# The opening of the x3 stage: a row broadcast moved into the stage before, a maximum given to GpSimd, the first gates ahead of a reciprocal, and k's first two pieces spread from SBUF

## The chip, the cores and the metric

The kernel runs on one core of a Trainium2 chip. The metric is the device time of one execution in microseconds (us). PE is the matrix engine, DVE the vector engine, ACT the activation engine, POOL is GpSimd, SP issues most DMAs. A core's program is one instruction stream per engine; the streams wait for each other by semaphores.

## The reference

Four residual layers follow one another on an image x of 256 x 256 positions with 128 channels: an attention along rows, two triangle multiplications, and a convolution block. Only the third layer, which makes x3 out of x2, matters here. Cut to what is computed (gn is a group norm over the image, whose statistics the kernel folds into weights):

```
z  = gn(x2)
zn = layernorm(z)                                  # over the 128 channels
a  = sigmoid(zn @ Wga + bga) * (zn @ Wla + bla)
b  = sigmoid(zn @ Wgb + bgb) * (zn @ Wlb + blb)
k  = einsum('bimc,bmjc->bijc', a, b)               # one 256x256x256 product per channel c
x3 = x2 + sigmoid(zn @ Wgo + bgo) * (layernorm(k) @ Wlo + blo)
```

## The kernel before

Data lies with the 128 channels on the partitions and the 65,536 positions along the free axis, cut into 32 pieces of 2048 positions (SC). Three stages make x3:

- **p5** (lines 1082 to 1217) makes a and b piece by piece and stores them to aD and bD. The row 1/sigma of zn goes to rs2D. Normalised pieces p5_zn live in three buffers. At its end PE multiplies pieces 30 and 31 for their output gates (line 1213), which are kept in the tiles gate_30 and gate_31.
- **p6**, "the planes" (lines 1249 to 1288), loops over the 128 channels c. Four channels of a and b are one load each (`load6`, tiles p6_A and p6_B, three buffers each). PE turns a's plane (`tri_turn`, line 1899), multiplies (`tri_multiply`, line 1910), ACT copies the product into p6_K (line 1278) and squares it into p6_sq (line 1280), DVE adds it to k1 (line 1281), POOL adds the square to k2 (line 1282). Every fourth step SP stores four channels to kD. k1 and k2 have 512 positions on each of the 128 partitions, so that piece s of 2048 positions lies on the partitions 4s to 4s+3.
- **p7** (lines 1309 to 1434) loops over the 32 pieces. For each: `gate7` multiplies x2 by a weight on PE, DVE adds a column and multiplies by the broadcast row 1/sigma (line 1347), ACT takes the sigmoid (line 1348); `spread_z` is POOL's broadcast of that row from one partition to all 128 (line 1331); `spread_k` is the broadcast of k's 1/sigma by PE (`broadcast_rows`, line 1073); `normalise_k` multiplies k by it on DVE (line 1326); `product7` multiplies by Wlo on PE; DVE combines it with the gate (line 1408), POOL adds x2 (line 1431), ACT takes sums for the next norm, SP stores x3.

Between p6 and the loop of p7 stands a prologue (lines 1375 to 1399). It turns k1 and k2 into 1/sigma of k: `k1 * k1 * (-1/D)` (line 1380), `k2 + k1` (1381), the maximum with 0 (1382), all on DVE; the square root on ACT (1383); the reciprocal on DVE into k1 (1384). k1 is stored to rkD and loaded again as rk, with piece s on the partitions s, 32+s, 64+s and 96+s, one quarter of 512 positions on each (lines 1385 to 1387). `broadcast_rows` makes four matmuls out of it: each takes the 32 partitions of its own quarter. Then the gates of pieces 0, 1 and 2 follow, and the loop runs three pieces ahead with its gates (AHEAD).

The order of the work in p5, p6 and p7 is written out by hand: each engine runs its instructions in the order of the text. All loads and stores of these stages are on SP's queue, in that order too.

The DVE instructions of the prologue stand in the text ahead of the gates, so DVE runs lines 1380 to 1384 before it takes the first gate out of the buffers p7_pm (two of them, in PSUM). `spread_z` has two buffers p7_rb in the pool p7.

Pools of SBUF tiles are laid one behind the other, a pool's tiles in the order of their first use, and a tile waits until what lay on its bytes has been read. Behind the two gate tiles (from byte 98016 of each partition) p5 has: p5_m2 2 KB, p5_var 4 KB, then p5_zn at 120544, 128736 and 136928, p5_a, p5_b. Buffers are taken in the order first, third, second: piece 29 lies on 128736, piece 30 on 120544, piece 31 on 136928. When p5 is closed, the pool rk takes its place from 114400: rk 2 KB, rs2_ 8 KB, k1 2 KB, k2 2 KB, to 128736. p6's tiles begin there, p6_A first, and later p7's: p7_junk, p7_k four times, p7_rb twice, p7_g five times, the first p7_g at 186208.

Of the kernel before, what the change touches and what calls it, by code (L numbers as in the profile page):

```python
# [9 lines left out]
F32 = mybir.dt.float32  # L10
AF = mybir.ActivationFunctionType
ALU = mybir.AluOpType
# [4 lines left out]
P = 128  # L17
N = 256
D = 128
T = N * N  # L20
SC = 2048
NSC = T // SC
CK = 512
# [9 lines left out]
def kernel(ctx: ExitStack, tc: tile.TileContext, a: dict, out: bass.AP):  # L33
    nc = tc.nc
# [116 lines left out]
    sel = const.tile([P, 32], F32, name="sel")  # L151
# [85 lines left out]
    with tc.tile_pool(name="x0", bufs=1, reuse_waits="tile") as xres, tc.tile_pool(name="p0", bufs=3, reuse_waits="tile") as sb:  # L237
# [168 lines left out]
        with tc.tile_pool(name="p1", bufs=2, reuse_waits="tile") as wk_sb, tc.tile_pool(name="p1ps", bufs=4, space=PSUM, reuse_waits="tile") as ps, tc.tile_pool(name="p1pe", bufs=1, space=PSUM, reuse_waits="tile") as psE:  # L406
# [7 lines left out]
            with tc.manual_schedule():  # L414
# [5 lines left out]
                for i, s in enumerate(order):  # L420
# [4 lines left out]
                    for c in range(4):  # L425
                        nc.tensor.matmul(
                            pr[32 * c : 32 * c + 32, :], lhsT=wt, rhs=xc[:, c * CK : (c + 1) * CK],
                            start=True, stop=True,
# [17 lines left out]
                    while len(sums) > (i < NSC - 1):  # L446
                        j, sq = sums.pop(0)
                        for c in range(4):
                            nc.tensor.matmul(
                                e2[32 * c : 32 * c + 32, :], lhsT=slide[:, 31 - j : 63 - j],  # L450
                                rhs=sq[:, c * CK : (c + 1) * CK], start=(j == order[0]), stop=(j == order[-1]),
# [24 lines left out]
    with tc.tile_pool(name="p2e", bufs=6, reuse_waits="tile") as eb, tc.tile_pool(name="p2c", bufs=1, reuse_waits="tile") as cs:  # L476
        triT = cs.tile([P, NH, 2, N], F32, name="triT")
        with tc.tile_pool(name="p2", bufs=2, reuse_waits="tile") as sb, tc.tile_pool(name="p2S", bufs=2, space=PSUM, reuse_waits="tile") as psS, tc.tile_pool(name="p2z", bufs=1, space=PSUM, reuse_waits="tile") as psZ, tc.tile_pool(name="p2M", bufs=3, space=PSUM, reuse_waits="tile") as psM, ExitStack() as by_hand:
# [182 lines left out]
            rb = psS.tile([P, 2, CK], F32, name="p2i_rb", tag="p2_S")  # L661
            for c in range(2):
                nc.tensor.matmul(
                    rb[:, c, :], lhsT=sel[32 * c : 32 * c + 32, 0:1].to_broadcast([32, P]),
                    rhs=rs0[32 * c : 32 * c + 32, :], start=True, stop=True,
# [173 lines left out]
    with x1_scope:  # L839
        with tc.tile_pool(name="p3", bufs=3, reuse_waits="tile") as sb, tc.tile_pool(name="p3ps", bufs=3, space=PSUM, reuse_waits="tile") as ps, tc.manual_schedule():  # L840
# [14 lines left out]
            for i, s in enumerate(order1):  # L855
                p1 = ps.tile([P, CK], F32, name="p3_1")
                p2 = ps.tile([P, CK], F32, name="p3_2")
                for pp, w in ((p1, v1), (p2, v2)):
                    for c in range(4):
                        nc.tensor.matmul(  # L860
                            pp[32 * c : 32 * c + 32, :], lhsT=w, rhs=xs[s][:, c * CK : (c + 1) * CK],
                            start=True, stop=True,
# [83 lines left out]
        with tc.tile_pool(name="p4", bufs=3, reuse_waits="tile") as sb, tc.tile_pool(name="p4psg", bufs=2, space=PSUM, reuse_waits="tile") as psg, tc.tile_pool(name="p4psz", bufs=2, space=PSUM, reuse_waits="tile") as psz, tc.manual_schedule():  # L946
            zs, gts, sums = {}, {}, []
# [42 lines left out]
            for i, s in enumerate(order):  # L990
# [5 lines left out]
                for c in range(4):  # L996
# [3 lines left out]
                        start=True, stop=True,  # L1000
# [67 lines left out]
    def broadcast_rows(psX, rows, s, name, tag="x"):  # L1068


        rb = [psX.tile([P, 2, CK], F32, name=name, tag=tag) for _ in range(2)]
        for c in range(4):
            nc.tensor.matmul(
                rb[c // 2][:, c % 2, :], lhsT=sel[32 * c : 32 * c + 32, s : s + 1].to_broadcast([32, P]),
                rhs=rows[32 * c : 32 * c + 32, :], start=True, stop=True,
            )
        return [t.rearrange("p c t -> p (c t)") for t in rb]
# [6 lines left out]
    gates = {s: rs2_pool.tile([P, SC], F32, name=f"gate_{s}") for s in (NSC - 2, NSC - 1)}  # L1084
# [143 lines left out]
    rk_pool = rs2_scope.enter_context(tc.tile_pool(name="rk", bufs=1, reuse_waits="tile"))  # L1228
    rk = rk_pool.tile([P, CK], F32, name="rk")
    rs2 = rk_pool.tile([P, SC], F32, name="rs2_")  # L1230

    def row7(s):
        at = 32 * (s % 4)
        return rs2[at : at + 1, :]

    def load_row7(s):
        if s < NSC - 2:
            nc.sync.dma_start(row7(s), rs2D[:, s * SC : (s + 1) * SC])

    k1 = rk_pool.tile([P, 2 * N], F32, name="k1")  # L1240
    k2 = rk_pool.tile([P, 2 * N], F32, name="k2")
    xs7 = {}

    def load7x(s):
        if s < NSC:
# [3 lines left out]
    with tc.tile_pool(name="p6", bufs=3, reuse_waits="tile") as sb, tc.tile_pool(name="p6ps", bufs=3, space=PSUM, reuse_waits="tile") as ps:  # L1249
        nc.vector.memset(k1, 0.0)  # L1250
        nc.gpsimd.memset(k2, 0.0)  # L1251
        with tc.manual_schedule():
            quads = {}

            def load6(q):
                if q < D // 4:
                    A = sb.tile([P, 4, 2 * N], F32, name="p6_A")
                    nc.sync.dma_start(A, aD[:, 4 * q : 4 * q + 4, :])
                    B = sb.tile([P, 4, 2 * N], F32, name="p6_B")
                    nc.sync.dma_start(B, bD[:, 4 * q : 4 * q + 4, :])  # L1260
                    quads[q] = A, B

            def turn6(c):
                return tri_turn(nc, ps, sb, quads[c // 4][0], c % 4, ident, nc.vector.tensor_copy)

            for q in range(3):
                load6(q)
            for s in range(4):
                load_row7(s)
            at = turn6(0)  # L1270
            for c in range(D):
                q = c // 4
                if c % 4 == 0:
                    K = sb.tile([P, 4, 2 * N], F32, name="p6_K")
                nxt = turn6(c + 1) if c + 1 < D else None
                pz = tri_multiply(nc, ps, at, quads[q][1], c % 4).rearrange("p t n -> p (t n)")
                at = nxt
                nc.scalar.copy(K[:, c % 4, :], pz)  # L1278
                sq = sb.tile([P, 2 * N], F32, name="p6_sq")
                nc.scalar.activation(sq, pz, AF.Square)  # L1280
                nc.vector.tensor_tensor(k1, pz, k1, ALU.add)  # L1281
                nc.gpsimd.tensor_tensor(k2, k2, sq, ALU.add)  # L1282
                if c % 4 == 3:
                    nc.sync.dma_start(kD[4 * q : 4 * q + 4, :].rearrange("c (p t) -> p c t", p=P), K)
                    del quads[q]
                    load6(q + 3)
                    if q >= D // 4 - 3:
                        load7x(q - (D // 4 - 3))
# [18 lines left out]
    g1 = const.tile([P, NSC + 1], F32, name="g1")  # L1307
    g2 = const.tile([P, NSC + 1], F32, name="g2")
    with tc.tile_pool(name="p7", bufs=2, reuse_waits="tile") as sb, tc.tile_pool(name="p7psX", bufs=2, space=PSUM, reuse_waits="tile") as psX, tc.tile_pool(name="p7psM", bufs=2, space=PSUM, reuse_waits="tile") as psM, tc.manual_schedule():
        ks, rks, rbs, gts = {}, {}, {}, dict(gates)  # L1310
        junk = sb.tile([P, SC], F32, name="p7_junk", bufs=1)
        AHEAD = 3

        def load7k(s):
            if s < NSC:
                ks[s] = sb.tile([P, SC], F32, name="p7_k", bufs=4)
                nc.sync.dma_start(ks[s], kD[:, s * SC : (s + 1) * SC])

        def spread_k(s):
            if s < NSC:  # L1320
                rks[s] = broadcast_rows(psX, rk, s, "p7_rk")

        def normalise_k(s, h):
            if s < NSC:
                hs = slice(h * H2, (h + 1) * H2)
                nc.vector.tensor_tensor(ks[s][:, hs], rks[s][h], ks[s][:, hs], ALU.mult)

        def spread_z(s):
            if s < NSC and s not in gates:
                rbs[s] = sb.tile([P, SC], F32, name="p7_rb")  # L1330
                nc.gpsimd.partition_broadcast(rbs[s], row7(s))

        def product7(src, w, h):
            pm = psM.tile([P, 2, CK], F32, name="p7_pm")
# [5 lines left out]
        def gate7(s, h):  # L1340
            if s < NSC and s not in gates:
                hs = slice(h * H2, (h + 1) * H2)
                if h == 0:
                    gts[s] = sb.tile([P, SC], F32, name="p7_g", bufs=5)
                pg = product7(xs7[s], wf2[:, 4, :], h)
                zg = gts[s][:, hs]
                nc.vector.scalar_tensor_tensor(zg, pg, gcol, rbs[s][:, hs], ALU.add, ALU.mult)
                nc.scalar.activation(zg, zg, AF.Sigmoid, bias=b2w[:, 4:5])
# [25 lines left out]

        load7k(0)
        load7x(3)
        spread_z(0)
        spread_z(1)

        nc.vector.scalar_tensor_tensor(k1, k1, -1.0 / D, k1, ALU.mult, ALU.mult)  # L1380
        nc.vector.tensor_tensor(k2, k2, k1, ALU.add)
        nc.vector.tensor_scalar(k2, k2, 0.0, None, ALU.max)
        nc.scalar.activation(k2, k2, AF.Sqrt, bias=epst, scale=1.0 / D)
        nc.vector.reciprocal(k1, k2)
        nc.sync.dma_start(rkD.rearrange("o (p t) -> p (o t)", p=P), k1)
        for c in range(4):
# [2 lines left out]
            load7k(s)  # L1389
        load7x(4)  # L1390
        for s in range(3):
            gate7(s, 0)
            gate7(s, 1)
            if s < 2:
                spread_z(s + 2)
                load_row7(s + 4)
        spread_k(0)
        normalise_k(0, 0)
# [1 line left out]
        for s in range(NSC):  # L1400
            load_row7(s + 6)
            load7k(s + 3)
            last = s == NSC - 1
            for h in range(2):
                hs = slice(h * H2, (h + 1) * H2)
                gate7(s + AHEAD, h)
                pl = product7(ks[s], w2[:, 5, :], h)
                nc.vector.scalar_tensor_tensor(
                    pl if last else gts[s][:, hs], pl, b2w[:, 5:6], gts[s][:, hs], ALU.add, ALU.mult
                )  # L1410
                if h == 0:
                    spread_k(s + 1)
                    spread_z(s + AHEAD + 1)
                normalise_k(s + 1, h)
                if last:
                    nc.vector.tensor_tensor(xs7[s][:, hs], pl, xs7[s][:, hs], ALU.add)
                    if h == 0:
                        finish7(s - 1)
                    for c in range(2):
                        k = 2 * h + c  # L1420
                        nc.vector.bn_stats(st7[:, k, :], xs7[s][:, k * CK : (k + 1) * CK])
                    nc.sync.dma_start(x3T[:, s * SC + h * H2 : s * SC + (h + 1) * H2], xs7[s][:, hs])
            del ks[s]
            if last:
                stats7()
            elif s == NSC - 2:
                for h in range(2):
                    hs = slice(h * H2, (h + 1) * H2)
                    nc.gpsimd.tensor_tensor(xs7[s][:, hs], xs7[s][:, hs], gts[s][:, hs], ALU.add)
            else:  # L1430
                nc.gpsimd.tensor_tensor(xs7[s], xs7[s], gts[s], ALU.add)
            if s and not last:
                finish7(s - 1)
            load7x(s + 5) if s + 5 < NSC else load9(s + 5 - NSC)
# [517 lines left out]
```

## Time and profile before

| what | us |
|---|---|
| median of three runs | 3272.09 |
| lowest and highest | 3267.91, 3276.04 |
| profiled execution: its own time | 3273.64 |
| profiled execution: span, first to last instruction | 3271.7 |
| last gate matmuls of p5 end, ACT takes them | 2333.36 |
| first turn of p6, first product of p6 on PE | 2335.88, 2338.47 |
| a step of p6 (line 1281, 128 of them) | 2.2465 |
| last step of p6 on DVE | 2628.75 |
| reciprocal, start and length | 2636.47, 3.35 |
| first matmul of gate 3, of gate 4 | 2651.66, 2659.90 |
| a step of p7, pieces 1 to 26 | 8.13 |
| first matmul after the x3 stage | 2906.44 |

Times within an execution are counted from its first instruction. A line of the timeline gives start, length, engine, source line, operation, out<-in, shape, how many were merged, and in brackets how long the engine had been idle and who ended that. A line of the table of stages gives for each engine its busy time and number of instructions, then the clock granted to PE (1.00 is full), the share of the DMA engines' time and GB/s.

### The profile page before, as it was taken

The numbers are of one execution on the slowest core, as the hardware profiler recorded it, in microseconds if no ns is written. First come the engines' busy times: TensorE is split into PE (matmuls) and PEld (weight loads), VectorE is DVE, ScalarE is ACT, GpSimd is POOL, SyncE is SP. The second block draws the span as 40 slices with busy tenths as digits, with TensorE's granted clock in tenths as the row PEclk, the third lists the DMA queues.
The fourth block names the chain that finished last, engine by engine and source line by source line (L and its number), as shares of the span: only waits on it lengthen the run. The fifth ranks groups of instructions, "written<-read, shape, count | busy, mean of one in ns | idle before, by whom it ended". The sixth has DMA issues, their size and how long they took to land. (4 is left out here: it accounts for less than half of the span.)

```text
span 3271.7 us, 51718 instructions
## 1 busy us (share of the span) xinstructions
PE 3040.7 (93%) x19792; PEld 1629.4 (50%) x19792; DVE 2248.5 (69%) x2540; ACT 2033.8 (62%) x2270; POOL 1773.4 (54%) x1019
## 2 busy tenths in 40 slices
PE   5678999999999999997799799999999989979998
PEld 4524555555555555552433244444699933324444
DVE  5626888888888888883456454454455588858887
ACT  3576777777777777763467545444344457757776
POOL 4055777777777777770268000000255568848887
PEclk8899999999999999998999899999999999989999
DMA  9982333333333333329679678666699989976775
GB/s 362 363 326 94 120 113 111 118 111 111 118 111 112 120 109 116 119 100 394 227 308 410 255 255 307 256 249 262 260 351 352 351 313 388 390 286 194 233 231 154
DMA packets 294802, 749.18 MB, mean 229 GB/s; under 512 B 71127, under 2 KB 142185, under 8 KB 245369
## 3 DMA queue, kind: packets, MB, share of 16 engines
q1 hardware_dynamic: 282671, 731.12, 61.9%
q0 software_dynamic: 9040, 13.17, 1.1%
q8 instruction: 158, 2.59, 0.3%
q10 hardware_dynamic: 2840, 1.54, 0.2%
q14 instruction: 93, 0.76, 0.1%
HBM read 458.07 MB, written 287.64 MB: 228 GB/s over the span
## 5 line engine op out<-in xcount | busy, mean ns | idle before, releaser
L555 DVE TENSOR_TENSOR p_e<-p_S,triT 128x1024 f32<-128x1024 f32 x512 | 609.4, 1212 | 144.8 <-PE p_S L545 144.8
L565 POOL TENSOR_TENSOR p_es<-p_e 128x1024 f32<-128x1024 f32 x256 | 602.8, 2367 | 126.2 <-issue 66.7
L563 ACT ACTIVATE p_e<-p_e,mbT 128x1024 f32<-128x1024 f32 x512 | 552.1, 1138 | 61.6 <-DVE p_e L555 61.6
L1154 PE MATMUL p_pm<-p_zn,wf 128*128 128x512 f32 x1040 | 448.7, 593 | 1.9 <-ACT p_a L1189 1.9
L530 PE MATMUL p_mm<-p_xn,w 128*128 128x512 f32 x768 | 405.1, 611 | 0.3 <-DVE p_v L525 0.3
L1154 PEld LDWEIGHTS p_pm<-p_zn,wf 128*128 128x128 f32 x1040 | 196.8, 190 | 253.9 <-issue 247.0
L545 PE MATMUL p_S<-p_q,p_k 32*128 32x256 f32 x4096 | 295.3, 401 | 3.5 <-DVE p_e L555 3.3
L1251 POOL MEMSET k<- 128x512 f32 x1 | 0.5, 525 | 522.4 <-PE p_pm L1154 522.4
L545 PEld LDWEIGHTS p_S<-p_q,p_k 32*128 32x128 f32 x4096 | 185.8, 184 | 159.5 <-PE p_mm L521 91.7
L504 POOL TENSOR_TENSOR p_xn<-p_xn,p_rs 128x1024 f32<-128x1024 f32 x63 | 151.3, 2401 | 205.1 <-ACT p_xn L499 108.4
L1910 PE MATMUL tp_z<-p_B,tp_at 128*128 128x256 f32 x1024 | 250.8, 388 | 0.9 <-DMA p_B<-bD 0.6
L578 PE MATMUL p_o<-p_e,p_v 128*32 128x256 f32 x4096 | 248.6, 383 | 0.0
L1282 POOL TENSOR_TENSOR k<-k,p_sq 128x512 f32<-128x512 f32 x128 | 163.1, 1274 | 136.5 <-ACT p_sq L1280 136.5
L1910 PEld LDWEIGHTS tp_z<-p_B,tp_at 128*128 128x128 f32 x1024 | 185.1, 191 | 21.9 <-DVE tp_at L1901 1.6
L530 PEld LDWEIGHTS p_mm<-p_xn,w 128*128 128x128 f32 x768 | 125.9, 190 | 104.4 <-issue 88.6
L1281 DVE TENSOR_TENSOR k<-tp_z,k 128x512 f32<-128x512 f32 x128 | 88.5, 692 | 127.0 <-ACT p_sq L1280 127.0
L578 PEld LDWEIGHTS p_o<-p_e,p_v 128*32 128x32 f32 x4096 | 120.3, 110 | 110.3 <-ACT p_g L536 41.5
L1278 ACT COPY p_K<-tp_z 128x512 f32<-128x512 f32 x128 | 74.9, 585 | 155.4 <-PE tp_z L1910 155.4
L536 ACT ACTIVATE p_g<-p_mm,bgh 128x512 f32<-128x512 f32 x128 | 87.9, 687 | 131.4 <-PE p_mm L530 131.4
L1193 DVE SCALAR_TENSOR_TENSOR p_b<-p_pm,b2w,p_b 128x1024 f32<-128x1024 f32 x64 | 82.2, 1284 | 121.7 <-PE p_pm L1154 107.3
L534 ACT ACTIVATE p_k<-p_mm,cqkg 128x512 f32<-128x512 f32 x128 | 87.9, 687 | 125.1 <-PE p_mm L530 124.9
L521 PEld LDWEIGHTS p_mm<-w,p_xn 128*128 128x128 f32 x1024 | 134.4, 191 | 61.1 <-issue 60.4
(386 smaller groups left out, 6101.2 us busy)
## 6 DMA issues: line engine op xcount, KB each, us to landing
p_x<-x2T SPq DMA_DIRECT2D x60, 1024.0 KB
x<-x1T SPq DMA_DIRECT2D x51, 1024.0 KB
p_x<-in_x_dram SPq DMA_DIRECT2D x32, 1024.0 KB
p_x<-xT SPq DMA_DIRECT2D x64, 512.0 KB
x2T<-x SPq DMA_DIRECT2D x32, 1024.0 KB
aD<-p_a SPq DMA_DIRECT2D x32, 1024.0 KB
bD<-p_b SPq DMA_DIRECT2D x32, 1024.0 KB
p_A<-aD SPq DMA_DIRECT2D x32, 1024.0 KB
```

The source lines that it names most:

```text
L504: nc.gpsimd.tensor_tensor(xn, xn, groups[g]["rs"], ALU.mult)
L521: nc.tensor.matmul(pm[:, k * D : (k + 1) * D], lhsT=t["xn"][:, b * P : (b + 1) * P], rhs=wf[:, 2 * D : 3 * D], start=True, stop=True,)
L530: nc.tensor.matmul(pm, lhsT=w, rhs=t["xn"][:, cs_], start=True, stop=True)
L545: nc.tensor.matmul(Ss[h // 2][:, h % 2, u, :], lhsT=t["k"][hp, r * N + u * P : r * N + (u + 1) * P], rhs=t["q"][hp, r * N : (r + 1) * N], ...
L555: nc.vector.tensor_tensor(e[:, :, 2 * p : 2 * p + 2, :].rearrange("p u h n -> p h u n"), Ss[p], triT[:, 2 * p : 2 * p + 2, :, :], ALU.add,)
L563: nc.scalar.activation(e[:, u, :, :], e[:, u, :, :], AF.Exp, bias=mbT[:, u, i : i + 1])
L565: nc.gpsimd.tensor_tensor(es, e[:, 0, :, :], e[:, 1, :, :], ALU.add)
L578: nc.tensor.matmul(t["o"][hp, r % 2, :], lhsT=t["v"][:, r * 2 + u, hp], rhs=e[:, u, h, :], start=(u == 0), stop=(u == 1),)
L1154: nc.tensor.matmul(pm[:, c, :], lhsT=wf2[:, i, :], rhs=zns[s][:, k * CK : (k + 1) * CK], start=True, stop=True)
L1281: nc.vector.tensor_tensor(k1, pz, k1, ALU.add)
L1282: nc.gpsimd.tensor_tensor(k2, k2, sq, ALU.add)
L1910: nc.tensor.matmul(pz[:, t, :], lhsT=at[:, u, t * P : (t + 1) * P], rhs=Bc[:, u, :], start=(u == 0), stop=(u == 1))
```

## The change

- The broadcast of row 0 is issued on POOL within p6, in step c = 112 of 128 (D - 16). Its buffer lies in the pool rk.
- `spread_z` takes the pool as an argument. Even pieces use one buffer p7_rb in the pool rk, odd ones one buffer in p7, in place of two in p7.
- In the prologue the broadcasts of rows 0 and 1 ahead of DVE's chain are gone; row 1's comes on POOL behind the maximum.
- The maximum with 0 goes from DVE to POOL.
- The gates of piece 0 (matmuls, line 1347 on DVE, sigmoid on ACT) stand ahead of the reciprocal in the text.
- k's 1/sigma for the pieces 0 and 1 is broadcast from k1 itself (`broadcast_k1`): four matmuls, all with the partitions 0 to 31 as their input, each selecting row 4s+c. Pieces from 2 on take rk as before.

```diff
@@ -1239,7 +1239,12 @@
-    xs7 = {}
+    xs7, rbs = {}, {}
+
+    def spread_z(s, pool):
+        if s < NSC and s not in gates:
+            rbs[s] = pool.tile([P, SC], F32, name="p7_rb", bufs=1)
+            nc.gpsimd.partition_broadcast(rbs[s], row7(s))
@@ -1280,6 +1285,8 @@
                 nc.gpsimd.tensor_tensor(k2, k2, sq, ALU.add)
+                if c == D - 16:
+                    spread_z(0, rk_pool)
                 if c % 4 == 3:
@@ -1316,19 +1323,23 @@
+        def broadcast_k1(s):
+            rb = [psX.tile([P, 2, CK], F32, name="p7_rk", tag="x") for _ in range(2)]
+            for c in range(4):
+                nc.tensor.matmul(
+                    rb[c // 2][:, c % 2, :], lhsT=sel[0:32, 4 * s + c : 4 * s + c + 1].to_broadcast([32, P]),
+                    rhs=k1[0:32, :], start=True, stop=True,
+                )
+            return [t.rearrange("p c t -> p (c t)") for t in rb]
+
         def spread_k(s):
             if s < NSC:
-                rks[s] = broadcast_rows(psX, rk, s, "p7_rk")
+                rks[s] = broadcast_rows(psX, rk, s, "p7_rk") if s > 1 else broadcast_k1(s)
-        def spread_z(s):
-            if s < NSC and s not in gates:
-                rbs[s] = sb.tile([P, SC], F32, name="p7_rb")
-                nc.gpsimd.partition_broadcast(rbs[s], row7(s))
@@ -1374,13 +1385,13 @@
         load7k(0)
         load7x(3)
-        spread_z(0)
-        spread_z(1)
-
         nc.vector.scalar_tensor_tensor(k1, k1, -1.0 / D, k1, ALU.mult, ALU.mult)
         nc.vector.tensor_tensor(k2, k2, k1, ALU.add)
-        nc.vector.tensor_scalar(k2, k2, 0.0, None, ALU.max)
+        nc.gpsimd.tensor_scalar(k2, k2, 0.0, None, ALU.max)
         nc.scalar.activation(k2, k2, AF.Sqrt, bias=epst, scale=1.0 / D)
+        spread_z(1, sb)
+        gate7(0, 0)
+        gate7(0, 1)
         nc.vector.reciprocal(k1, k2)
         nc.sync.dma_start(rkD.rearrange("o (p t) -> p (o t)", p=P), k1)
@@ -1389,10 +1400,11 @@
         load7x(4)
         for s in range(3):
-            gate7(s, 0)
-            gate7(s, 1)
+            if s:
+                gate7(s, 0)
+                gate7(s, 1)
             if s < 2:
-                spread_z(s + 2)
+                spread_z(s + 2, (rk_pool, sb)[s % 2])
                 load_row7(s + 4)
@@ -1410,7 +1422,7 @@
                     spread_k(s + 1)
-                    spread_z(s + AHEAD + 1)
+                    spread_z(s + AHEAD + 1, (rk_pool, sb)[s % 2])
                 normalise_k(s + 1, h)
```

More of the change, by code (lines that the diff above doesn't have):

```diff
@@ L1309 @@
     with tc.tile_pool(name="p7", bufs=2, reuse_waits="tile") as sb, tc.tile_pool(name="p7psX", bufs=2, space=PSUM, reuse_waits="tile") as psX, tc.tile_pool(name="p7psM", bufs=2, space=PSUM, reuse_waits="tile") as psM, tc.manual_schedule():
-        ks, rks, rbs, gts = {}, {}, {}, dict(gates)
+        ks, rks, gts = {}, {}, dict(gates)
         junk = sb.tile([P, SC], F32, name="p7_junk", bufs=1)
```

## The prediction

> **What bounds the kernel now.** The chain that ended last holds 3 us, so I read in order of time. First the table of stages: is the x3 loop bound by something that a head start moves?
>
> ```profile
> core 0: us, PE busy (x) PEld busy (x) DVE busy (x) ACT busy (x) POOL busy (x), PEclk, DMA share, GB/s
> 2700.00:2740.00 40.00, 40.00 (x120) 15.55 (x119) 35.40 (x31) 31.35 (x30) 33.57 (x11) 1.00 1.01 388
> ```
>
> PE has no gap. In the list of waits of 2640 to 2910 no matmul or product waits for a load of k or x2, so a gain ahead of the loop moves it whole (8.13 us a step), with the join behind it. The DMA queues are full too (388 GB/s), but each load is issued by the same waits and moves along. So two stretches count. The first is the loop's opening, on DVE, POOL and PE:
>
> ```profile
> 2629.48 1.20 DVE L1380 SCALAR_TENSOR_TENSOR k<-k 128x512 f32<-128x512 f32 x1
> 2630.78 2.47 DVE L1381 TENSOR_TENSOR k<-k,k 128x512 f32<-128x512 f32 x1
> 2633.28 2.40 DVE L1382 TENSOR_SCALAR k<-k 128x512 f32<-128x512 f32 x1
> 2636.47 3.35 DVE L1384 RECIPROCAL k<-k 128x512 f32<-128x512 f32 x1 [0.79 <-ACT k L1383]
> 2639.74 2.38 DVE L1347 SCALAR_TENSOR_TENSOR p_g<-p_pm,gcol,p_rb 128x1024 f32<-128x1024 f32 x2
> ```
> ```profile
> 2630.14 5.27 POOL L1331 PARTITION_BROADCAST p_rb<-rs__17911  x2
> ```
> ```profile
> 2629.50 3.70 PE L1337 MATMUL p_pm<-p_x,wf 128*128 128x512 f32 x8 [1.90 <-DVE k L1281]
> 2640.99 9.68 PE L1337 MATMUL p_pm<-p_x,wf 128*128 128x512 f32 x16 [7.79 <-DVE p_g L1347]
> 2650.59 1.14 PE L1073 MATMUL p_rk<-rk,sel 32*128 32x512 f32 x8
> 2651.66 1.99 PE L1337 MATMUL p_pm<-p_x,wf 128*128 128x512 f32 x4
> ```
>
> DVE's two ops beside the broadcasts end just as a broadcast ends; the same maximum takes 0.43 elsewhere (line 1130). PE fills both p7_pm buffers, then idles 7.79 until DVE, behind the reciprocal, takes the first gate. After that its clock is 0.50 until 2645.8. rk isn't on this path: k's broadcast starts the moment the last gate matmul ends.
>
> The second stretch is p6's opening (SP, then PE), which the diff doesn't name:
>
> ```profile
> 2328.90 0.33 SPq L1258 DMA_DIRECT2D p_A<-aD  x1
> 2332.94 0.33 SPq L1260 DMA_DIRECT2D p_B<-bD  x1
> ```
> ```profile
> 2335.88 1.98 PE L1899 MATMUL tp_a<-ident,p_A 128*128 128x128 f32 x8 [2.56 <-DMA p_A<-aD]
> 2338.47 3.75 PE L1910 MATMUL tp_z<-p_B,tp_at 128*128 128x256 f32 x8 [0.61 <-DMA p_B<-bD]
> ```
>
> PE waits there for A's first load, then for B's. The 127 steps that follow take 2.2465 us each without slack (2343.44 to 2628.75), so a late opening is paid whole.
>
> **The opening of the loop, step by step**, on the clock of before; gains are earlier.
>
> 1. Broadcast of row 0 into p6, at c = 112. POOL works 1.27 of 2.25 us a step; 2.30 more puts it 1.33 behind, made good in two steps of 0.97 idle. p6_sq has three buffers, so ACT's squares aren't held: 0. Without that cover it costs 2.3.
> 2. DVE's chain. L1380 keeps its end, 2630.68 (POOL's last k2 add ends 2630.12). L1381 no longer stands beside a broadcast: 0.6 (L1380 took 0.56 once the add had ended), ends 2631.4. The maximum on POOL has no row; memset and copy of that shape take 0.53 and 0.60, the two-input add 1.27, the far end is a broadcast's 2.30. I take 1.27: ends 2632.8, square root 2633.6. Behind it on POOL stands the broadcast of row 1, done 2635.1 and wanted at 2637.9; on ACT the sigmoid's table load. Even 2.30 costs 0.1.
> 3. First gates ahead of the reciprocal: they wait for PE, at 2631.4 and 2633.25, and run 1.28 each to 2634.5. The reciprocal stands behind them, 3.35 to 2637.9, 1.9 earlier; so the store of rkD and SP's queue behind it (rk, k(1), k(2), x(4), row 4) move 1.9 earlier. Does it suffer beside POOL's broadcasts? 256 elements from PSUM take 1.75, 512 from SBUF 3.35, one slope, so I take 0; the far end is one broadcast, 2.3.
> 4. PE. Buffers come free at 2632.7 and 2634.5, so gate 1's matmuls run to 2636.5; PE then idles 2.66 until DVE takes gate(1,0) at 2637.9 to 2639.2. Warm, gate 2's two halves follow in 3.8 and k's broadcast starts at 2642.9 instead of 2650.59: gain 7.7. Row 2's broadcast waits for gate(0,1) and is done at 2637.4, row 3's at 2642.7; both are hidden.
> 5. Is PE warm? Before, its cold spell cost 6.28 − 3.82 = 2.46. Gaps of 2.48, 2.56, 2.58, 2.60 and 2.63 us in this trace were followed by clocks of 1.00, 0.50, 0.82, 0.68 and 0.50 over 1.5 us, mean 0.70: loss 0.6 × 2.46 = 1.5, ends 0 and 2.46. The Trainium skill (TensorE: Matmul & The Clock Gate, Why this matters for your kernels) says that only gaps over about 3 us cool the array; by it this term would be 0 and the sum 1.5 lower. The trace's 2.56 at 0.50 speaks against it.
> 6. Broadcasts of k for pieces 0 and 1 from k1. Today the four matmuls lie on four row quarters and the next matmul starts 1.07 after the first. The new ones all use rows 0 to 31. At line 663 two quarters' four records, at 0.50 clock, start in pairs, 254.5 and 255.5: quarters overlap, one quarter's two passes don't. So eight passes at 0.43 (the spacing of 512 columns): 3.43, 2.36 more, twice: 4.7 lost. Bounds: 0 and 4.7. The same page (Part 3: Packing small matmuls) gives 3.07 times for four quarters, an estimate of 3.28 and a loss of 4.4: it speaks against this part as well. Normalising (2644.8, 2646.5) and the second broadcast's psX buffers don't hold PE beyond that.
> 7. Loads. k(0) and x(3), issued 2633.4 and 2633.8, have landed by 2641; wanted at 2644.8 and 2646. k(1) is issued at 2641.8; wanted at 2651. Row 4 took 8.9; 2643.1 + 8.9 + 2.3 = 2654.3, wanted at 2658: hidden.
>
> Gain: 7.7 − 1.5 − 4.7 = 1.5, ends 0.5 and 7.7 (−1.8 with a held reciprocal).
>
> **The opening of p6.** p7_rb's new buffer lies in the rk pool, 8 KB that move p6's tiles up. The first p6_A buffer goes from 128736 to 136928. The piece of p5_zn on 128736 was s = 29, long read; on 136928 it is s = 31, read by the last gate matmuls until 2333.3 (ACT starts on them at 2333.36). So A's first load, at the head of SP's queue, waits from 2328.90 to 2333.36, and B's (then 2333.75 instead of 2332.94), four more loads and four rows wait behind it. B's move alone gives the low end, 0.8; A's 4.46 the high one. Between: k(4) at 2660.09 was 0.95 from issue to first data in an idle queue, 1 MB takes 2.5 at 420 GB/s, and PE started 1.55 after the data ended: A lands at 2338.4 instead of 2335.88, B 2.5 behind at 2340.9 instead of 2338.45. Loss 2.5. Behind p6 only tiles long read change places: gate 0 lies where it lay, now over tp_at.
>
> **Sum.** −1.5 + 2.5 = +1.0 us. The profiled execution (3273.64, of which 1.94 outside the span) would become 3274.6; it stands 1.55 above the median of the three, so 3273.1 beside 3272.09.
>
> **Rivals.**
> - *Quarters don't matter*: the same-quarter matmuls overlap as today's. The spacing at line 663 speaks against it, no row here has four on one quarter. Gain 6.2: 3268.4.
> - *A's load is no worse*: the queue makes up for it and B's 0.8 is all; B did gate the first product. 3271.4.
> - *The maximum on POOL is slow*: tensor_scalar has no row on POOL since its library was loaded. If it costs L, the square root, the reciprocal and gate 1 wait; above L = 2.2 each us is lost whole. At L = 13 the time is 11.8 above before, 3283.9; it ends slower by over 0.3% from L = 11. Against it: no POOL elementwise row of this shape is over 1.29.
> - *The change doesn't shorten the opening*: a cold PE and a held reciprocal, gain −1.8, with p6's 2.5: 3276.4.
>
> **How the numbers follow.** Likeliest 0.62 (its own range 3270 to 3275); overlap 0.10; A no worse 0.12; no shortening 0.13; slow maximum 0.03. The runs of before span 3267.9 to 3276.0, which I add in part: 3267 to 3279. What this kernel's measurement can tell from no change is about 0.3%, 9.8 us, more than every case but one gives: same 0.95, slower 0.03, faster 0.02.
>
> **What would show it.** Right: A's first load issued at about 2333.4 and the first product at about 2341; L1381 at 0.6 us; the reciprocal ending 8.4 us after the first gate matmul begins (10.3 before); L1073's first two groups 3.4 us long, the others 1.1; 8.13 us a step unchanged. Wrong: A's issue still at 2328.9, k's first broadcast within 1.1 us, or a step that waits for x2, since the head start meets a queue that was already full.

## The result: 705 us slower, and the profile after

| | before | after |
|---|---|---|
| median, us | 3270.00 (4 runs) | 3975.28 (4 runs) |
| lowest and highest | 3266.34, 3276.04 | 3974.20, 3985.37 |
| profiled execution: own time, span | 3273.64, 3271.7 | 3974.44, 3972.7 |
| mean granted clock of PE | 0.965 | 0.893 |
| from ACT's take of p5's last gate matmuls to PE's first matmul behind the x3 stage | 573.1 | 884.3 |
| from there to the end of the span | 365.3 | 762.3 |

The ratio is 1.2159 (95% interval 1.2141 to 1.2177). The last two rows are read from the timelines: line 1215's last start (2333.36 and 2326.15) to line 197's first start behind the stage (2906.44 and 3210.40). I use these two lengths below, since what stands ahead of them is the same work in every kernel and yet took between 2320 and 2335 us in the profiles (7.2 us less in the changed kernel's than in that of before). They say where the time came from: 311 us in the x3 stage, and 397 us in the last stage, which the change doesn't touch.

The page's busy line of the changed kernel, first, is no help. POOL's busy time before was 1773.4 us:

```profile
PE 3180.3 (80%) x19792; PEld 1698.6 (43%) x19792; DVE 2245.9 (57%) x2539; ACT 2041.1 (51%) x2270; POOL 1778.3 (45%) x1020
```

Except for PE no engine works more than 8 us longer (ACT 7.3, POOL 4.9), and PE does the same 19792 matmuls at a lower clock. So the engines are waiting. The table of stages of the changed kernel, for the same 40 us as the line that the prediction opens with:

```profile
2700.00:2740.00 40.00, 20.58 (x48) 8.04 (x48) 14.61 (x12) 13.14 (x13) 13.64 (x4) 0.75 0.43 159
```

48 matmuls where there were 120, at a clock of 0.75 instead of 1.00, and 159 GB/s instead of 388. The list of waits of the changed kernel (who waited for whom: sum, times, longest) names one engine at the root of it:

```profile
DVE p_z L1627 <- POOL p_eb L1604: 356.4, 31, 15.2
...
DVE p_g L1358 <- POOL p_rb L1247: 257.0, 27, 11.1
...
POOL p_eb L1604 <- issue: 217.4, 32, 9.7
...
POOL p_rb L1247 <- issue: 149.6, 25, 6.4
POOL p_x L1443 <- issue: 145.3, 20, 7.8
```

Before, the first two of these waits (there lines 1615 and 1347) were small:

```profile
DVE p_z L1615 <- POOL p_eb L1592: 5.6, 6, 3.4
...
DVE p_g L1347 <- POOL p_rb L1331: 2.7, 1, 2.7
```

DVE now waits for POOL's broadcasts, and POOL waits for "issue": for nothing that the profile shows another engine or a transfer to deliver. POOL's timeline, first in the loop of before, then in the changed kernel, shows where that begins:

```profile
2706.93 2.29 POOL L1331 PARTITION_BROADCAST p_rb<-rs__17911  x1
2710.40 4.57 POOL L1431 TENSOR_TENSOR p_x<-p_x,p_g 128x2048 f32<-128x2048 f32 x1 [1.18 <-DVE p_g L1408]
```

```profile
2634.98 1.52 POOL L1390 TENSOR_SCALAR k<-k 128x512 f32<-128x512 f32 x1 [9.55 <-issue]
2642.41 4.48 POOL L1247 PARTITION_BROADCAST p_rb<-rs__17911  x2 [5.91 <-issue]
...
2692.05 4.51 POOL L1443 TENSOR_TENSOR p_x<-p_x,p_g 128x2048 f32<-128x2048 f32 x1 [7.13 <-issue]
2702.41 2.30 POOL L1247 PARTITION_BROADCAST p_rb<-rs__17911  x1 [5.86 <-issue]
2711.76 4.52 POOL L1443 TENSOR_TENSOR p_x<-p_x,p_g 128x2048 f32<-128x2048 f32 x1 [7.04 <-issue]
2722.20 2.31 POOL L1247 PARTITION_BROADCAST p_rb<-rs__17911  x1 [5.93 <-issue]
```

The maximum itself takes 1.52 us. Ahead of it POOL stands still for 9.55 us. In the loop it then stands still 5.8 to 6.4 us ahead of each broadcast and 6.9 to 7.8 us ahead of most adds (some of these waits are put down to DVE or a DMA instead of "issue"), where it had 1.2 us to spare. What it does there is in the list of the instructions of a line, the sequencer's rows included (POOLq; count, shortest/median/longest in ns, first and last start). Three answers of the changed kernel, for the maximum, the broadcast and the add:

```profile
L1390 POOLq MODIFY_POOL_CONFIG  x2: 11/11/11, 2625.4 to 2625.4; - x2
...
L1247 POOLq MODIFY_POOL_CONFIG  x52: 1/1/15, 2636.7 to 3157.7; - x52
...
L1443 POOLq MODIFY_POOL_CONFIG  x52: 127/129/129, 2656.6 to 3165.6; - x52
```

MODIFY_POOL_CONFIG is the row that line 98's `load_library` leaves; there are two for one load. Behind each such pair in these stages POOL's next operation starts 5.6 us later or more. So POOL's code library is exchanged ahead of the maximum, then 26 times ahead of a broadcast and 26 times ahead of an add. In the last stage the broadcast of line 1604 has 62 such rows, the small operations of lines 1551, 1577 and 1647 have 28, 30 and 4. Together these are 230 rows, 115 exchanges behind line 98, where the kernel before has none; 705 us / 115 is 6.1 us each.

The step of the loop follows: broadcast 2.30, wait 7.04, add 4.52, wait 5.93, together 19.8 us, which is the distance of the broadcasts at 2702.41 and 2722.20. Against 8.13 that is 11.7 more, times 26 some 304 of the 311 us. In the last stage the broadcasts came every 9.84 us before (2934.3 to 3239.2, 32 of them) and come every 22.35 us now (3246.5 to 3939.4): 12.5 more, times 31 is 388 of the 397.

The rest of the prediction's rows, in the changed kernel. The opening of p6 on SP's queue and PE:

```profile
2326.15 0.33 SPq L1263 DMA_DIRECT2D p_A<-aD  x1
```
```profile
2333.72 3.75 PE L1922 MATMUL tp_z<-p_B,tp_at 128*128 128x256 f32 x8 [0.61 <-DMA p_B<-bD]
```

ACT took the last gate at 2326.15 here: A's first load is issued at that same moment, and the first product stands 7.57 behind it, against 5.11 before. And the opening of the loop, DVE and then PE:

```profile
2626.08 0.69 DVE L1389 TENSOR_TENSOR k<-k,k 128x512 f32<-128x512 f32 x1
2626.83 1.28 DVE L1358 SCALAR_TENSOR_TENSOR p_g<-p_pm,gcol,p_rb 128x1024 f32<-128x1024 f32 x1
...
2637.29 3.35 DVE L1395 RECIPROCAL k<-k 128x512 f32<-128x512 f32 x1 [7.46 <-ACT k L1391]
2644.75 2.48 DVE L1358 SCALAR_TENSOR_TENSOR p_g<-p_pm,gcol,p_rb 128x1024 f32<-128x1024 f32 x2 [4.11 <-POOL p_rb L1247]
```
```profile
2624.80 7.13 PE L1348 MATMUL p_pm<-p_x,wf 128*128 128x512 f32 x16 [1.90 <-DVE k L1286]
2646.09 6.60 PE L1348 MATMUL p_pm<-p_x,wf 128*128 128x512 f32 x8 [14.15 <-DVE p_g L1358]
2652.62 4.51 PE L1329 MATMUL p_rk<-k,sel 32*128 32x512 f32 x8
```

The sum with k1 takes 0.69 and the first gates stand ahead of the reciprocal, as planned. But PE then stands still for 14.15 us, because the reciprocal and the broadcast of row 1 both wait for POOL.

The start of the same profile bears this out, and shows that the two rows alone aren't a price:

```profile
1.44 0.29 POOL masks.py:199 TENSOR_SCALAR_AFFINE_SELECT ident<-ident 128x128 f32<-128x128 f32 x1 [0.29 <-POOL ones L77]
...
12.15 0.86 POOL L111 DMA_DIRECT2D L_conv_ln_w_sb<-in_L_conv_ln_w_dram  x1 [8.54 <-issue]
```

The kernel's first affine_select has two rows of MODIFY_POOL_CONFIG in every kernel. In the three whose last rows stand ahead of an add (the changed kernel, and below the kernel before with only the maximum on POOL and the kernel whose extra load ran at 69 us) it follows after 0.29 us; in the eight others, before among them, where line 98's library was the last one loaded, it waits 9.2 to 11.5 us. That is as if an execution begins with the library that the one before it left, and pays only where the operation isn't in it; which execution came before isn't on record.

**Theory and rivals.** Theory: the engine of the maximum is the whole cause. The operation isn't in the library that is loaded; the load for it also sends away the broadcast, and what is brought in for the broadcast is followed by a load for the add, and so on to the end. Rivals: another part of the change has a share (the broadcast in p6, the new order); a tensor_scalar leaves POOL slow whatever it holds; the lower clock or a queue that builds up carries a share from stage to stage.

### The profile page after: what moved, and what is told of

It reads as the page before. It is cut to its first block, busy times and chain, and to the rows that moved or that the text cites. A ratio compares the mean times of both kernels' runs of the same rounds, so it can differ in the third digit from the quotient of the medians.

```text
span 3972.7 us, 51951 instructions
## 1 busy us (share of the span) xinstructions
PE 3180.3 (80%) x19792; PEld 1698.6 (43%) x19792; DVE 2245.9 (57%) x2539; ACT 2041.1 (51%) x2270; POOL 1778.3 (45%) x1020
## 5 line engine op out<-in xcount | busy, mean ns | idle before, releaser
L1348 PE MATMUL p_pm<-p_x,wf 128*128 128x512 f32 x240 | 163.9, 824 | 250.1 <-DVE p_g L1358 248.2
L1497 PE MATMUL p_pp<-p_x,w1f 128*32 128x512 f32 x258 | 59.7, 1010 | 277.4 <-DVE p_z L1627 267.6
L1627 DVE TENSOR_TENSOR p_z<-p_zp,p_eb 128x1024 f32<-128x1024 f32 x64 | 75.3, 1219 | 356.4 <-POOL p_eb L1604 356.4
L1358 DVE SCALAR_TENSOR_TENSOR p_g<-p_pm,gcol,p_rb 128x1024 f32<-128x1024 f32 x60 | 76.9, 1283 | 302.2 <-POOL p_rb L1247 257.0
L1443 POOL TENSOR_TENSOR p_x<-p_x,p_g 128x2048 f32<-128x2048 f32 x30 | 135.6, 4524 | 196.5 <-issue 145.3
L1359 ACT ACTIVATE p_g<-p_g,b2w 128x1024 f32<-128x1024 f32 x60 | 68.8, 1148 | 260.7 <-DVE p_g L1358 255.4
L1348 PEld LDWEIGHTS p_pm<-p_x,wf 128*128 128x128 f32 x240 | 57.1, 253 | 334.9 <-DVE p_g L1358 277.8
L1501 ACT ACTIVATE p_st<-p_pp,s 128x512 f32<-128x512 f32 (+1 forms) x33 | 22.6, 686 | 337.2 <-PE p_pp L1497 331.8
```

The costliest lines, as they stand in the source:

```text
L1348: nc.tensor.matmul(pm[:, c, :], lhsT=w, rhs=src[:, k * CK : (k + 1) * CK], start=True, stop=True)
```

## Experiments on the maximum

**The changed kernel with the maximum on DVE.**

```diff
-        nc.gpsimd.tensor_scalar(k2, k2, 0.0, None, ALU.max)
+        nc.vector.tensor_scalar(k2, k2, 0.0, None, ALU.max)
```

> The changed kernel with the maximum back on DVE, all else as changed. Theory A (the maximum is an instruction that the GpSimd code resident since line 98 does not hold; it has GpSimd's code exchanged, and from then on every turn between broadcast and add exchanges it again): no MODIFY_POOL_CONFIG behind line 98, 8.13 us a step of the x3 loop, time 3268 to 3275 (the other terms of the prediction: 2.5 lost at p6's opening, about 4.7 on k's first two broadcasts, about 6 won on the first gates, some of that given back because row 1's broadcast again stands beside DVE's add). Theory B (row broadcasts with one buffer in each of two pools, or the rest of the change, hold the loop): stays above 3900, 20 us a step.

Measured: 3272.25 us (3265.61 to 3281.53), ratio to before 1.0009 (0.9996 to 1.0021). The two lengths are 578.2 and 366.9 us. With the rest of the change in place, all of the 705 us but some 3 are gone.

**The kernel before with only the maximum on POOL.**

```diff
-        nc.vector.tensor_scalar(k2, k2, 0.0, None, ALU.max)
+        nc.gpsimd.tensor_scalar(k2, k2, 0.0, None, ALU.max)
```

> Theory (the engine of the maximum is the whole cause): the kernel before with nothing changed but the maximum on GpSimd shows the same exchanges ahead of the maximum, of each broadcast and of each run of adds, and takes 3970 to 3990 us. Rival (the 704 us need another part of the change too, the row 0 broadcast in the planes or the new order): it stays within 20 us of 3271, with at most one exchange behind the start.

Measured: 3968.27 us, just under the expected range, ratio 1.2132 (1.2110 to 1.2154); lengths 881.7 and 763.2. The rows of the library (here line 1331 is the broadcast, 1431 the add) are as many as in the changed kernel:

```profile
L1331 POOLq MODIFY_POOL_CONFIG  x52: 1/2/28, 2632.5 to 3148.7; - x52
...
L1431 POOLq MODIFY_POOL_CONFIG  x52: 127/129/129, 2652.9 to 3156.6; - x52
```

One instruction of 1.53 us, moved from one engine to another, costs the whole time, with none of the other parts there.

**The library loaded again right behind the maximum.**

```diff
         nc.gpsimd.tensor_scalar(k2, k2, 0.0, None, ALU.max)
+        nc.gpsimd.load_library(library_config.all_libraries[10])
```

> The changed kernel with the code library of the start loaded again right behind the maximum. Theory (the loop pays because the library that the maximum brought in is followed by ones that hold either the broadcast or the add, never both): only the exchange for the maximum and the one back remain, some 9.6 and 5.9 us on GpSimd; gate 2 begins some 22 us after the last step of the planes as in the changed kernel, against 11.9 with the maximum on VectorE, so 3281 to 3291 us, and a step of the loop takes 8.13 again. Rival (a tensor_scalar leaves GpSimd slow for all that follows, whichever library it holds): about 3975.

Measured: 3285.68 us (3279.96 to 3290.63), ratio 1.0039 (1.0027 to 1.0050). Two exchanges are left behind line 98. POOL's timeline, with the maximum, the broadcasts and the first turns of the loop:

```profile
2643.77 1.53 POOL L1390 TENSOR_SCALAR k<-k 128x512 f32<-128x512 f32 x1 [9.63 <-issue]
2650.45 4.49 POOL L1247 PARTITION_BROADCAST p_rb<-rs__17911  x2 [5.14 <-issue]
...
2681.74 2.29 POOL L1247 PARTITION_BROADCAST p_rb<-rs__17911  x1
2685.22 4.58 POOL L1444 TENSOR_TENSOR p_x<-p_x,p_g 128x2048 f32<-128x2048 f32 x1 [1.19 <-issue]
2689.89 2.29 POOL L1247 PARTITION_BROADCAST p_rb<-rs__17911  x1
```

9.63 us away and 5.14 back, and then broadcast and add follow each other as before the change, 8.15 us apart: the library of line 98 holds both, and the operation leaves nothing slow behind. So of the changed kernel's 705 us some 690 are for not having had that library put back. The other 13 aren't all the maximum's: against the kernel with the maximum on DVE the way through the stage is 9.0 us longer (587.2 to 578.2), and the lower clock in that kernel's profile, below, hides up to 3.4 more. Gate 2 began 21.4 us after DVE's last step of p6 (2632.76 to 2654.12), as expected. The way through the stage was 587.2, which is 14.1 above before, and it splits into 2.6 for p6 (below) and 11.5 for the loop's opening.

**The library loaded again only ahead of the last stage.**

```diff
+    nc.gpsimd.load_library(library_config.all_libraries[10])
     rs2_scope.close()
```

> The changed kernel with the library loaded again only ahead of the last stage. By the two traces the way from the last gate of p5 to the statistics behind the x3 stage is 884.3 us against 573.1 before (+311), and what follows 762.3 against 365.3 (+397). Theory (each exchange is paid where it stands and nothing else is slower): the last stage takes 365 again, the x3 stage keeps its +311, so 3572 to 3590. Rival (part of the loss is a lower clock or a queue that builds up and is carried over): the last stage stays over 380.

Measured: 3972.81 us, ratio 1.2148 (1.2125 to 1.2171), lengths 880.8 and 763.6. A miss, and it says nothing on the theory: the load had not been where it stood in the text. Its rows in the list of the line's instructions:

```profile
L1463 POOLq MODIFY_POOL_CONFIG  x2: 37/37/37, 69.0 to 69.0; - x2
```

It ran 69 us after the start. The call of a load names no tile, so no tile ties it to the adds that it is to follow, and here, outside of the stages with an order written out by hand, it went ahead. In the hand-written order of the x3 stage it stays in its place:

```diff
                     nc.gpsimd.tensor_tensor(xs7[s][:, hs], xs7[s][:, hs], gts[s][:, hs], ALU.add)
+                nc.gpsimd.load_library(library_config.all_libraries[10])
             else:
```

> The same test as the run before with the load of the library at the place it was meant for, behind GpSimd's last add of the x3 stage (there it had gone to 69 us after the start, where the library was in already). Theory (each exchange is paid where it stands and nothing else is slower): what follows the statistics behind the x3 stage takes 365 us again (762.3 in the changed kernel, 365.3 before), the x3 stage keeps its +311, so 3572 to 3590. Rival (part of the loss is a lower clock or a queue that builds up and is carried over): what follows stays over 380.

Measured: 3573.11 us (3571.79 to 3574.45), ratio 1.0938 (1.0920 to 1.0957), lengths 878.9 and 366.6. The table of stages of this kernel, 40 us in the x3 loop and 40 us in the last stage:

```profile
2700.00:2740.00 40.00, 20.96 (x48) 8.10 (x48) 14.61 (x12) 12.97 (x12) 13.66 (x4) 0.76 0.43 161
3250.00:3290.00 40.00, 39.07 (x143) 17.02 (x144) 33.53 (x39) 27.59 (x36) 34.88 (x27) 0.96 0.53 157
```

The x3 loop is as slow as in the changed kernel (48 matmuls, clock 0.76), and behind the load the last stage is at full work and takes 366.6, against 365.3 before. So each exchange is paid where it stands and nothing is carried over; the low clock goes with PE's waiting.

What stays open: whether the library that comes in for the broadcast really lacks the add. The slow kernels show that a load stands ahead of each and takes its time; what those libraries hold, no trace lists.

## Experiments on the rest of the change

With the maximum on DVE the other steps can be read without the exchanges. Counted from DVE's last step of p6 (line 1281, or 1286 or 1287 in the others), the broadcast of k's row for piece 0 began on PE at 21.84 us before, and that for piece 2, where all kernels are in the loop's steady step, at 34.68 (2628.75 to 2663.43).

| maximum on DVE, and | from last gate to first product of p6 | from p6's last step to broadcast 0 | to broadcast 2 | whole x3 way |
|---|---|---|---|---|
| (before) | 5.11 | 21.84 | 34.68 | 573.1 |
| nothing else | 7.32 | 15.52 | 36.81 | 578.2 |
| k's pieces 0 and 1 from rk | 7.48 | 15.44 | 28.93 | 569.9 |
| p6_K laid first | 4.83 | 15.44 | 33.39 | 570.9 |

**k's row for pieces 0 and 1 by the four quarters of rk again.**

```diff
-                rks[s] = broadcast_rows(psX, rk, s, "p7_rk") if s > 1 else broadcast_k1(s)
+                rks[s] = broadcast_rows(psX, rk, s, "p7_rk")
```

> As max_on_dve, and k's first two pieces broadcast from rk by four row quarters as before. If four matmuls of one quarter run one after another (3.6 us against 1.1), this is 4 to 5 us faster than max_on_dve; if the spread from SBUF is free or hidden, the same within 1 us.

Measured: 3265.51 us (3260.39 to 3271.92), ratio 0.9990 (0.9978 to 1.0002); that is 6.7 us under the median with the maximum on DVE, where 4 to 5 were expected (the lower clock in the other kernel's profile, below, may have a share). PE in this kernel, then in the kernel with broadcasts from one quarter (p6_K laid first, which PE ran at full clock too; line 1330 is its broadcast of k1):

```profile
2641.33 1.80 PE L1073 MATMUL p_rk<-rk,sel 32*128 32x512 f32 x8
2643.06 1.98 PE L1348 MATMUL p_pm<-p_x,wf 128*128 128x512 f32 x4
...
2646.69 1.14 PE L1073 MATMUL p_rk<-rk,sel 32*128 32x512 f32 x8
2647.76 1.98 PE L1348 MATMUL p_pm<-p_x,wf 128*128 128x512 f32 x4
```
```profile
2636.21 3.69 PE L1330 MATMUL p_rk<-k,sel 32*128 32x512 f32 x8
2639.84 1.98 PE L1349 MATMUL p_pm<-p_x,wf 128*128 128x512 f32 x4
...
2643.47 3.70 PE L1330 MATMUL p_rk<-k,sel 32*128 32x512 f32 x8
2647.09 1.98 PE L1349 MATMUL p_pm<-p_x,wf 128*128 128x512 f32 x4
```

From a broadcast's start to the next matmul: 3.63 and 3.62 us on one row quarter; 1.73 (the first, whose four quarters start over 0.68 us instead of 0.02) and 1.07 on four. From broadcast 0 to broadcast 2 it is 17.95 us with the one and 13.49 with the other: this part of the change costs 4.5 us.

**p6's store tiles laid first.** The first p6_K is allocated ahead of p6_A, so that p6_A comes to lie elsewhere than on the last p5_zn.

```diff
+            K0 = sb.tile([P, 4, 2 * N], F32, name="p6_K")
...
-                    K = sb.tile([P, 4, 2 * N], F32, name="p6_K")
+                    K = sb.tile([P, 4, 2 * N], F32, name="p6_K") if c else K0
```

> As max_on_dve, with p6's K tiles laid ahead of its A tiles, so that A's first load no longer lies on the normalised piece 31. Expected: A's first load issued about 4.5 us earlier against the last gate's matmuls of p5, first product of p6 2.5 us earlier, time 2.5 us below max_on_dve. If p6's opening does not count, the same.

Measured: 3267.71 us (3260.76 to 3276.35), ratio 1.0001 (0.9989 to 1.0012). The median is 4.5 us under the kernel without it, where 2.5 were expected, but the intervals of the two ratios overlap; the trace shows the step itself. ACT took the last gate at 2325.89; SP and PE in this kernel:

```profile
2321.40 0.33 SPq L1264 DMA_DIRECT2D p_A<-aD  x1
```
```profile
2330.72 3.59 PE L1923 MATMUL tp_z<-p_B,tp_at 128*128 128x256 f32 x8 [1.61 <-DMA p_B<-bD]
```

The load is issued 4.49 us ahead of ACT's take, as it was before (4.46), and the first product stands 4.83 behind it instead of 7.32: the place of p6_A was worth 2.5 us.

This table holds one thing that I had not looked for. With nothing else changed, broadcast 2 comes 3.4 us later than with p6_K laid first, though both issue the same work and PE had waited no longer than 1.9 us in either. The table of stages shows PE's clock (the last but two of the columns), 4 us at a time, with the maximum on DVE and nothing else:

```profile
2644.00:2648.00 4.00, 4.00 (x7) 1.39 (x6) 2.45 (x2) 0.93 (x1) 0.00 (x0) 0.66 1.02 430
2648.00:2652.00 4.00, 4.00 (x6) 1.42 (x5) 1.28 (x1) 0.16 (x1) 0.26 (x1) 0.50 1.02 428
```

and the same stretch of the kernel with p6_K laid first, 28 us of it from the end of p6:

```profile
2621.00:2649.00 28.00, 23.82 (x53) 9.50 (x54) 21.36 (x16) 10.97 (x10) 10.64 (x5) 1.00 0.91 350
```

The clock fell to 0.50 for some 6 us in one profiled execution, which had been at 0.57 from 2628 to 2632 too, and stayed at 1.00 from 2618 to 2656 in the three others with the maximum on DVE (k's pieces from rk, p6_K laid first, and the second of the versions below). One profile each doesn't say what decides it.

**A version that beats both kernels.** Of the change: the broadcast of row 0 in p6, and the first gates ahead of the reciprocal. Not of it: k's pieces from k1. Added: p6_K laid first. Once with the sum on POOL and the maximum on ACT (each an operation that needs no other library), once with both on DVE:

```diff
-        nc.vector.tensor_tensor(k2, k2, k1, ALU.add)
-        nc.gpsimd.tensor_scalar(k2, k2, 0.0, None, ALU.max)
+        nc.gpsimd.tensor_tensor(k2, k2, k1, ALU.add)
+        nc.scalar.activation(k2, k2, AF.Relu)
```

> Row 0's broadcast in p6, first gates ahead of the reciprocal, k from rk, K tiles first, and in place of the maximum on GpSimd: the addition k2 + k1 on GpSimd (an add, as in p6) and the maximum as a Relu on ACT ahead of the square root. No exchange of code. Expected 5 to 7 us below before (3263 to 3266 where before is 3270). If the opening of the loop is held by something else, such as rk's way through memory, within 2 us of before.

> Row 0 broadcast in the planes, first gates ahead of the reciprocal, k's row for all pieces from rk on four row quarters, the planes' store tiles laid first, the add and the maximum both on VectorE: from the parts measured (the way from p5's last gate to the statistics 573.1 before, 569.9 with rk and A's load late, that load some 2.3 earlier) 567.5, so 5.5 us under before: 3264 to 3267. With the add on GpSimd and the maximum on ScalarE the same way took 566.9. Rival (the add beside a broadcast, 2.46 us, holds the square root so that the first gates move back): no gain over before.

Measured: 3261.32 us (3256.99 to 3267.60), ratio 0.9975 (0.9964 to 0.9985), with the sum on POOL; 3264.99 us (3259.49 to 3272.26), ratio 0.9984 (0.9974 to 0.9993), with both on DVE. The ways through the x3 stage are 566.9 and 566.6 us, 6.2 and 6.5 under before; the two can't be told apart, and both are faster than the kernel before, by a quarter of a per cent and less. With the sum on POOL the loop's opening is the one that the prediction drew, but for where the maximum runs. PE there:

```profile
2630.13 7.13 PE L1349 MATMUL p_pm<-p_x,wf 128*128 128x512 f32 x16 [1.90 <-DVE k L1287]
2640.03 5.35 PE L1349 MATMUL p_pm<-p_x,wf 128*128 128x512 f32 x8 [2.76 <-DVE p_g L1359]
2645.31 1.27 PE L1073 MATMUL p_rk<-rk,sel 32*128 32x512 f32 x8
```

PE waits 2.76 us, gate 2 takes 5.28 where it takes 3.63 at full clock (line 1349 in the kernel with p6_K laid first, 2632.58 to 2636.21), and broadcast 0 begins 15.92 behind p6's last step (2629.39).

## Why the prediction was wrong

It said 3273.1 with a range of 3267 to 3279; the time is 3975.3.

- **The step that failed is item 2's price of the maximum on POOL.** It took 1.27 us from the two-input add, with 0.53 and 2.30 as ends, and concluded that "Even 2.30 costs 0.1". The operation's own row is 1.52, within those ends. Not in any of the rows that were taken was the exchange of the library: 9.55 us ahead of it, and 114 exchanges behind it.
- **The rival "The maximum on POOL is slow" had the right place and half of the mechanism.** It said that tensor_scalar has no row on POOL since its library was loaded, and charged that once. For one exchange there and one back its scale was right, in part by luck, since its L of 13 was read from no row: the run with the library put back ended 12.8 us above before (0.39%), where the rival gave 11.8. But it took for granted that POOL would be as before once the maximum was done. It weighed that rival by the durations of operations that were in the library ("no POOL elementwise row of this shape is over 1.29"), which says nothing on one that isn't.
- **The price stood in the profile of before.** POOL's timeline of its first 18 us, which the prediction doesn't use:

```profile
10.39 0.28 POOL masks.py:199 TENSOR_SCALAR_AFFINE_SELECT ident<-ident 128x128 f32<-128x128 f32 x1 [9.22 <-issue]
...
17.63 0.86 POOL L111 DMA_DIRECT2D L_conv_ln_w_sb<-in_L_conv_ln_w_dram  x1 [5.08 <-issue]
```

  An operation of 0.28 us waits 9.22 us for "issue", with two MODIFY_POOL_CONFIG rows ahead of it (1.1 us), and behind line 98's load, whose rows are at 12.8, POOL stands for 5.08. That is an exchange away and one back, 14.3 us, and the run with the library put back repeats both (9.63 and 5.14). An estimate from these rows for a foreign operation here, one that the loaded library doesn't hold, is 8.5 us (9.22 and the 1.5 that it took itself, less the rival's 2.2 to spare), and there was a question to ask that the prediction didn't: the kernel's text doesn't load the library again, so what does the next broadcast find? The Trainium skill (GPSIMD Engine Reference, Instruction dispatch) states about 6 us for the first call of a freshly loaded kernel; the 5.8 to 6.4 ahead of the loop's broadcasts agree, the 6.9 to 7.8 ahead of its adds and the 9.55 ahead of the maximum are more.
- **Item 1, row 0 in p6 at no cost: right.** From p6's first product to its last step 290.45 us with k's pieces from rk, 291.06 with nothing else, 290.28 before; the second holds a product of 2.54 that takes 1.9 in its neighbours. Nothing of the 2.3 shows.
- **Items 3 to 5, the gain ahead of k's broadcast: right in size, with the exchange left out.** A wait of 2.66 on PE, 7.7 gained, 1.5 lost on a cold PE, together 6.2. In the kernel with the sum on POOL and the maximum on ACT the wait is 2.76, the cold gate loses 1.65 and broadcast 0 begins 5.9 earlier (21.84 to 15.92). With the maximum on DVE the first two gates end 1.7 later, the wait is shorter and gate 2 runs at full clock (3.63), and it is 6.3. The cold term was read from five gaps, and the trace of before has two more of that size, 2.50 and 2.63 us, both followed by 0.50 (the clock had been under 1.00 ahead of them); with these the mean is 0.64 and the term 1.8. And it covered gate 2 alone: behind broadcast 0 one profile lost 3.4. In the changed kernel itself broadcast 0 begins 28.56 after p6's last step (2624.06), as the reciprocal starts 7.46 late and row 1's broadcast holds the next gate for another 4.11.
- **Item 6, four matmuls on one row quarter: right.** 3.43 was taken for a broadcast, 3.62 measured; 4.7 for the two, 4.5 measured.
- **The opening of p6: right.** A's load was to wait for ACT's last take and to cost 2.5. It is issued in that moment, and the first product came 7.57 behind it instead of 5.11, 2.46 late; with p6_K laid first this is gone.
- **The signs named ahead.** A's load, the first product, the sum at 0.6 (0.69) and the two long broadcasts came as said. The reciprocal's end, 8.4 us behind the first gate matmul, came at 15.8, and the step of 8.13 at 19.8: both by the exchange. The kernel with the maximum on DVE stands 2.9 us above before (1.0009; 0.9996 to 1.0021), which holds the sum of +1.0 but is too wide to confirm it. In its profile the way through the x3 stage is 5.1 us longer, and the clock that fell behind broadcast 0 has 3.4 of them.

## What to carry to other kernels

Before an operation is given to GpSimd, ask whether the code library that is loaded at that point holds it: look for the same operation behind the last load in the trace, and where there is none, price an exchange from the "issue" time behind the MODIFY_POOL_CONFIG rows, and ask who loads the old library again. A single foreign operation can turn every later change between two kinds of operations into an exchange, to the end of the program. Where a gain of a few us is worth it, an engine that shows no such exchange in these traces (here DVE or ACT for the maximum), or an operation that the loaded library holds, gets it without that risk.

## What the runs showed of the hardware

- An exchange of GpSimd's code doesn't count as busy time: POOL's busy time grew by 4.9 us while the kernel lost 705. It shows as "issue" in most of the waits, and as MODIFY_POOL_CONFIG among the sequencer's rows. The rows stand there also where nothing is paid (0.29 us ahead of the first affine_select in three kernels).
- Its length isn't one figure: 9.2 to 11.5 us ahead of the first affine_select where it is paid; 9.4, 9.55, 9.63 and 9.9 ahead of the maximum in four kernels (11.7 in a fifth, put down to a DMA); in the loop 5.8 to 6.4 ahead of a broadcast and 6.9 to 7.8 ahead of an add. It isn't set by what is loaded alone: line 98's load stands 5.0 to 5.1 us where an exchange has just come ahead of it, and 8.5 to 10.0 in the three kernels where it is the first one paid. What decides it stays open.
- A load of a library isn't tied to the operations around it in the text. Outside of a hand-written order it ran at 69 us, some 3,100 us ahead of the stage that it was meant for.
- PE's clock went down to 0.50 twice at the x3 loop's opening in one execution, where its longest waits were 1.90 and 1.92 us, and not in three others, with waits of up to 1.90 there.
